# Loading the first weights ahead of later tokens, and laying the first projections one by one among the first attention steps

## The chip, the cores and the metric

The kernel runs on one core of a Trainium2 chip. The time is the device time of one execution in microseconds (us). A time of a kernel is the median over several runs. A profile is taken of one further execution, which has its own time.

## The reference

The computation is one transformer layer on 2048 tokens of width 256, all in 32-bit floats: a differential attention block and a feed-forward block, each between a layer norm in front and a layer norm behind, with the input added back. The part that the change touches is the front of the attention block.

```python
qkv = layernorm(x) @ Wqkv_w.T + Wqkv_b           # 2048 x 4096
q, k, v = split(qkv, [2048, 1024, 1024])         # 16 q heads, 8 k heads of 128; 4 v heads of 256
p1, p2 = softmax of causal (q . k) / sqrt(128)   # the two halves of each pair of heads
o = (p1 - lam * p2) @ v
o = rmsnorm(o) * subln_w * (1 - LAMBDA_INIT)
x = x + layernorm(o @ out_w.T + out_b)
```

The feed-forward block multiplies by signs, does a Walsh-Hadamard transform, and has gate, up and down matrices of 1024 hidden columns. The kernel folds the transforms into the weights.

## The kernel before, in words

**Tiling.** Tokens lie in 16 tiles of 128, and in four blocks of 512. The heads lie in four groups; a group has four q heads, two k heads and one v head of 256 columns. `qT`, `kT` and `vt` hold one group, and `xnT` holds the normalised input, transposed, with the 256 features in two chunks on the partitions.

**Stages.** Block 0 of x is loaded as four tiles, by SP and ACT in turn; blocks 1 to 3 (512 KB each) by SP, into a pool of three buffers. `load_qkv(0, ...)` loads the group's weights `wq` in four pieces of 256 KB, all from ACT's queue, in the order k, q heads 0 and 1, q heads 2 and 3, v; the v bias comes from POOL's queue. `colv` (biases and scales, 27 KB) is loaded by POOL and scaled there by `load_lambdas`, which then issues the loads of the lambdas, of `wo` and of the output bias. `norm_first` and `norm_in(b)` normalise a block on VectorE (statistics, then a power on POOL, then one subtract-and-multiply per tile). `turn_in(b)` transposes a block on TensorE in eight transposes and copies the two chunks to `xnT`, one on ACT and one on VectorE. `project_heads(g, nb, j2)` projects two heads of block nb in four matmuls of 512 columns into one PSUM tile and evicts the two halves with the bias; `j2` 0 and 1 are q, 2 is k. With `both=False` both halves are evicted by ACT, else the second by VectorE. `project_values(g, nb)` does v for a block in eight matmuls of 256 columns and one eviction on VectorE.

**Attention steps.** A unit is a token tile of one group (both halves of it for tiles 0 to 7). Each step of the main loop brings a new unit: half 0 of its `scores`, `exponentials`, then `combine` of the unit before it (which mixes the two softmaxes, transposes in blocks and sends the result through DRAM), then half 1 of the scores, then `values` (output `po`) of the unit three steps back, then `project_out`.

**What sets the order.** The order on each engine is the order in which the program issues the work; it is written out by hand. Dictionaries `before`, `mid`, `between` and `after` hold, for each step, the functions that are called at four places in it; `put` and `put_block` fill them. Around the change, `before` of step 0 runs ahead of the first scores, `mid` and `between` after `combine`, and `after` at the end of the step. Scores, projections and transposes take their PSUM tiles in turn from the pool `ps_s`, which has three buffers, so a tile waits until the tile three places earlier has been read. The pool `ps_o` has two buffers and serves `po` and `pout`. `WARM` matmuls on the identity run at the very start.

Of the kernel before, what the change touches and what calls it, by code (L numbers as in the profile page):

```python
# [10 lines left out]
F32 = mybir.dt.float32  # L11
# [5 lines left out]
P = 128  # L17
# [13 lines left out]
LAMBDA_INIT = 0.8 - 0.6 * math.exp(-0.3 * 1)  # L31
SCALE = D ** (-0.5)
LAG = 3
WARM = 12
MASKED = 1e30
HIGHEST = 3e38

# [7 lines left out]
NCOL = 54  # L45
# [3 lines left out]
def kernel(  # L49
# [14 lines left out]
    nc = tc.nc  # L64

    const = ctx.enter_context(tc.tile_pool(name="const", bufs=1))
    ident = const.tile([P, P], F32, name="ident")
    make_identity(nc, ident)

# [5 lines left out]
    mhalf = const.tile([P, 4], F32, name="mhalf")  # L75
    nc.gpsimd.memset(mhalf, -0.5)

    colv = const.tile([P, NCOL], F32, name="colv")
    nlam = const.tile([P, 1], F32, name="nlam")

    acc = const.tile([P, NT, HID], F32, name="acc")
# [1 line left out]
    def rstd_of(pool, src, n, tag):  # L83

        st = pool.tile([P, 4, 6], F32, tag="st" + tag, name="st" + tag)
        mv = pool.tile([P, 4, 2], F32, tag="mv" + tag, name="mv" + tag)
        for t in range(n):
            nc.vector.bn_stats(st[:, t, :], src[t] if isinstance(src, list) else src[:, t, :])
            nc.vector.bn_aggr(mv[:, t, :], st[:, t, :])
        ve = pool.tile([P, 4], F32, tag="ve" + tag, name="ve" + tag)  # L90
        nc.vector.tensor_scalar(ve[:, :n], mv[:, :n, 1], EPS, None, ALU.add)
        rstd = pool.tile([P, 4], F32, tag="rs" + tag, name="rs" + tag)
        nc.gpsimd.tensor_tensor(rstd[:, :n], ve[:, :n], mhalf[:, :n], ALU.pow)
        return mv, rstd

    def normalise(dst, src, mv, rstd, t):
        nc.vector.tensor_scalar(
            dst, src, mv[:, t, 0:1], rstd[:, t : t + 1], ALU.subtract, ALU.mult
        )
# [7 lines left out]
    with ExitStack() as actx:  # L107
# [6 lines left out]
        ps_s = actx.enter_context(tc.tile_pool(name="ps_s", bufs=3, space=PSUM))  # L114
        ps_o = actx.enter_context(tc.tile_pool(name="ps_o", bufs=2, space=PSUM))
# [3 lines left out]
        qT = [qkp.tile([P, NT, 2, 2, 64], F32, name=f"q{m}") for m in range(2)]  # L119
# [6 lines left out]
        xnT = xtp.tile([P, 2, S], F32, name="xnT")  # L126
        wsrc = wqkvT.rearrange("(c p) o -> p c o", p=P)
        loaded = {}

        def load_qkv(g, engine, pieces=1):  # L130

            wq = xtp.tile([P, 2, 1024], F32, tag="wq", name=f"wq_{g}")
            vb = xtp.tile([P, 256], F32, tag="vb", name=f"vb_{g}")
            step = 512 // pieces
            parts = [(512, 2048 + g * 256, 256)]
            parts += [(lo, g * 512 + lo, step) for lo in range(0, 512, step)]
            parts += [(768, 3072 + g * 256, 256)]
            for lo, at, n in parts:
                engine.dma_start(wq[:, :, lo : lo + n], wsrc[:, :, at : at + n])
            nc.gpsimd.dma_start(vb, vbias[:, ts(g, 256)].to_broadcast([P, 256]))  # L140
            loaded[g] = wq, vb

# [18 lines left out]
                    ALU.mult,  # L161
                )

        def project_heads(g, nb, j2, both=True):

            wq, _ = loaded[g]
            cols4 = ts(nb, 512)
            pp = ps_s.tile([P, 1024], F32, tag="sc", name=f"pp_{g}_{nb}_{j2}")
            for h in range(2):
                j = 2 * j2 + h  # L170
                for c in range(2):
                    nc.tensor.matmul(  # L172
                        pp[:, ts(h, 512)],
                        lhsT=wq[:, c, ts(j, P)],
                        rhs=xnT[:, c, cols4],
                        start=(c == 0),
                        stop=(c == 1),
                    )
            for h in range(2):
                j = 2 * j2 + h  # L180
                col = g * 4 + j if j < 4 else H + g * 2 + j - 4
                bias = colv[:, C_QKB + col : C_QKB + col + 1]
                src = pp[:, ts(h, 512)]
                if j < 4:
                    dst = qT[h][:, ts(nb, 4), :, j2, :].rearrange("d t s q -> d (t s) q")
                    src = src.rearrange("d (t q) -> d t q", q=64)
                else:
                    dst = kT[h][:, cols4]
                scale = -SCALE if j < 4 else 1.0
                if h == 0 or not both:  # L190
                    nc.scalar.activation(dst, src, AF.Identity, bias=bias, scale=scale)
                else:
                    nc.vector.tensor_scalar(dst, src, scale, bias, ALU.mult, ALU.add)
# [262 lines left out]
        xsm = pstack.enter_context(tc.tile_pool(name="xsm", bufs=2, side="right"))  # L456
        xts = []
        for b in range(NB):
            xt = xin.tile([P, 4, HID], F32, tag="xt", name=f"xt_{b}")
            if b:  # L460
                nc.sync.dma_start(xt, x4[b])
            else:

                for t in range(4):
                    (nc.sync, nc.scalar)[t % 2].dma_start(xt[:, t, :], x4[0][:, t, :])
                load_qkv(0, nc.scalar, pieces=2)
            xts.append(xt)
        nc.gpsimd.dma_start(colv, cols)

        def warm_up():  # L470

# [1 line left out]
            for k in range(WARM):  # L473
                nc.tensor.matmul(warm[:, :P], lhsT=ident, rhs=ident, start=True, stop=True)

        def norm_first():

            xt = xts[0]
            done = None
            for t in range(4):  # L480
                ln = rstd_of(xsm, xt[:, t : t + 1, :], 1, f"x{t}")
                if done:
                    normalise(xt[:, t - 1, :], xt[:, t - 1, :], *done, 0)
                done = ln
            normalise(xt[:, 3, :], xt[:, 3, :], *done, 0)

        def norm_in(b):
            xt = xts[b]
# [248 lines left out]
        pieces = ffn_pieces()  # L737
# [14 lines left out]
        before, mid, between, after = {}, {}, {}, {}  # L752

        def put(where, step, f, *args, **kw):
            where.setdefault(step, []).append(lambda: f(*args, **kw))

        def put_block(where, steps, g, nb, parts, both=True):
            for step, part in zip(steps, parts):
                if part == 3:
                    put(where, step, project_values, g, nb)  # L760
                else:
                    put(where, step, project_heads, g, nb, part, both=both)


        put(before, 0, warm_up)
        put(before, 0, norm_first)
        put(before, 0, load_lambdas)
        put(before, 0, turn_in, 0)
        put_block(before, [0] * 2, 0, 0, [2, 0], both=False)
        put(before, 0, norm_in, 1)  # L770
        put(before, 0, lambdas)
        put_block(before, [0], 0, 0, [1], both=False)
        put(before, 0, turn_in, 1)
        put_block(mid, [0], 0, 0, [3], both=False)
        put(mid, 0, norm_in, 2)
        put_block(mid, [0] * 2, 0, 1, [0, 1], both=False)
        put(between, 0, turn_in, 2)
        put_block(between, [0] * 2, 0, 1, [2, 3], both=False)
        put(mid, 1, norm_in, 3)
        put_block(mid, [1] * 2, 0, 2, [0, 1], both=False)  # L780
        put_block(between, [1, 1], 0, 2, [2, 3], both=False)
        put(mid, 2, turn_in, 3)
        put_block(between, [2, 3, 3, 4], 0, 3, range(4), both=False)
        put(after, 4, pstack.close)
        for g in range(1, NG):
            end = place[g, NT - 1, 0]
            put(after, end - 12, load_qkv, g, nc.sync)
            put(after, end + LAG + 2, load_wo, g)
            put(mid, end + LAG + 3, scale_wo, g)
            if g == 1:  # L790

                for nb in range(3):
                    put_block(between, [end + 5 - 2 * nb, end + 6 - 2 * nb], g, nb, [0, 1])
                put_block(before, [end] * 2, g, 3, [0, 1])
                for nb in range(4):
                    put_block(before, [end], g, nb, [2])
                    put_block(after, [end + 2], g, nb, [3])
            else:
                put_block(between, [end - 5, end - 4, end - 4, end - 3], g, 3, range(4))
                put_block(between, [end - 3, end - 3, end - 2, end - 2], g, 2, range(4))  # L800
                put_block(between, [end - 2, end - 1, end - 1], g, 1, range(3))
                put_block(after, [end - 1, end], g, 1, [3])
                put_block(before, [end], g, 0, [2])
                put_block(between, [end, end + 1], g, 0, [0, 1])
                put_block(after, [end + 2], g, 0, [3])
# [36 lines left out]
        at = lambda k: units[k] if 0 <= k < len(units) else None  # L842
# [92 lines left out]
```

## Time and profile before

| What | Value |
|---|---|
| Median of 3 runs | 1466.45 us (1466.3 to 1468.71) |
| The profiled execution's own time | 1470.85 us |
| Its span in the trace | 1469.1 us |
| Mean granted TensorE clock | 0.997 |
| TensorE busy | 1445.6 us |
| VectorE busy | 1035.0 us |
| ACT busy | 517.4 us |
| POOL busy | 359.5 us |

In the profile, PE is TensorE's matmul row, PEld its weight loads, DVE is VectorE, ACT is ScalarE, POOL is GpSimd, SP is the engine that issues most DMAs. A 32-bit matmul of the program shows as two matmuls in the trace, so `x24` is twelve of the program. A chain line has the start, the length and what ran, followed back from the last instruction of the execution. The lines are L165 to L193 for `project_heads`, L201 and L208 for `project_values`, L260 to L286 for the scores, L376 for `values`, L500 to L502 for the transposes of x.

### The profile page before, as it was taken

What the parts mean: (1) busy time and instruction counts of PE and PEld (TensorE: products, weight loads), DVE (VectorE), ACT (ScalarE), POOL (GpSimd) and SP (SyncE); (2) the same over time, 40 slices, a digit from 0 to 9 for tenths busy, and PEclk for the clock granted to TensorE, in tenths of its full rate; (3) what the DMA queues carried; (4) which work ended last, traced back from release to release, by engine and by line L of the source; (5) the groups of instructions that cost most, each with busy time, mean ns of one, the idle gap of its engine ahead of it and who ended that gap; (6) DMA issues with size and microseconds to landing.
All of it is one profiled execution on the core that took longest, in us unless ns stands there. A gap on an engine that the chain in (4) does not pass through costs nothing.

```text
span 1469.1 us, 17573 instructions
## 1 busy us (share of the span) xinstructions
PE 1445.6 (98%) x5464; PEld 1036.9 (71%) x5464; DVE 1035.0 (70%) x2408; ACT 517.4 (35%) x1121; POOL 359.5 (24%) x684
## 2 busy tenths in 40 slices
PE   8999999999999999999999999999999999999998
PEld 5567776666767677676677776675677767888887
DVE  4479788756576888744867779545877888756774
ACT  2354333323232334322433334223433454531211
POOL 2016734642006861011101111111111121121110
PEclk9999999999999999999999999999999999999999
DMA  3059899965486889831698898631999998522000
GB/s 116 22 129 193 184 200 219 175 129 117 84 186 154 159 183 210 175 91 49 137 183 176 176 203 172 140 75 30 208 205 187 199 183 174 142 76 61 29 23 15
DMA packets 494716, 204.50 MB, mean 139 GB/s; under 512 B 390960, under 2 KB 491840, under 8 KB 494624
## 3 DMA queue, kind: packets, MB, share of 16 engines
q1 hardware_dynamic: 490576, 193.65, 62.9%
q0 software_dynamic: 2512, 8.29, 2.2%
q10 hardware_dynamic: 1536, 1.44, 0.3%
q8 instruction: 45, 0.74, 0.2%
q14 instruction: 47, 0.39, 0.1%
HBM read 107.90 MB, written 95.42 MB: 138 GB/s over the span
## 4 chain that ended last, share of the span: by engine, by line
PE 91%; DVE 6%; ACT 1%; DMA 1%; issue 1%; ACTq 0%; POOL 0%; POOLq 0%; DVEq 0%
PE po L376 30%; PE sc L260 28%; PE pp L172 11%; PE pout L441 7%; PE gu L660 7%; PE pv L201 4%; PE pd L690 4%; DVE e L275 2%; DVE e L333 1%; DVE e L352 1%; DMA wq<-in_wqkvT 1%; DVE e L286 0%; PE tx L647 0%; DVE xo L420 0%; DVE cf L328 0%
## 5 line engine op out<-in xcount | busy, mean ns | idle before, releaser
L260 PE MATMUL sc<-k,q 128*128 128x512 f32 (+7 forms) x1280 | 479.5, 520 | 9.7 <-DVE last L286 3.7
L376 PE MATMUL po<-v,pt 128*128 128x256 f32 x2176 | 485.4, 379 | 0.0
L376 PEld LDWEIGHTS po<-v,pt 128*128 128x128 f32 x2176 | 425.9, 196 | 57.1 <-issue 9.3
L260 PEld LDWEIGHTS sc<-k,q 128*128 128x128 f32 x1280 | 236.5, 190 | 229.6 <-issue 183.8
L301 ACT ACTIVATE e<-e,last 128x192 f32<-128x192 f32 (+28 forms) x256 | 299.6, 1171 | 219.8 <-DVE last L286 204.2
L275 DVE TENSOR_SCALAR_CACHE_REDUCE e<-sc 128x1024 f32<-128x1024 f32 (+15 forms) x248 | 231.2, 932 | 189.6 <-PE sc L260 188.8
L401 POOL TENSOR_TENSOR u<-ss,ed 128x1 f32<-128x1 f32 (+1 forms) x96 | 18.3, 191 | 764.6 <-ACT po L390 764.4
L387 ACT COPY osb<-po 128x256 f32<-128x256 f32 (+1 forms) x96 | 42.6, 444 | 459.3 <-PE po L376 451.9
L172 PE MATMUL pp<-xnT,wq 128*128 128x512 f32 x384 | 173.2, 601 | 4.1 <-DMA wq<-in_wqkvT 2.4
L352 DVE STREAM_TRANSPOSE e<-e 128x768 f32<-128x768 f32 (+7 forms) x192 | 172.3, 937 | 6.7
L333 DVE SCALAR_TENSOR_TENSOR e<-e,cf,e 128x64 f32<-128x64 f32 (+31 forms) x128 | 173.8, 1378 | 3.4
L172 PEld LDWEIGHTS pp<-xnT,wq 128*128 128x128 f32 x384 | 73.1, 193 | 89.0 <-issue 84.3
L441 PE MATMUL pout<-wo,oT 128*128 128x256 f32 x512 | 120.9, 379 | 0.0
L275 DVE TENSOR_SCALAR_CACHE_REDUCE e<-sc,mx 128x320 f32<-128x320 f32 (+13 forms) x128 | 97.2, 759 | 21.0 <-PE sc L260 7.9
L441 PEld LDWEIGHTS pout<-wo,oT 128*128 128x128 f32 x512 | 97.3, 190 | 12.8
L673 ACT ACTIVATE hT<-gu,colv 128x256 f32<-128x256 f32 x64 | 30.4, 475 | 132.6 <-PE gu L660 91.0
L286 DVE CUSTOM_DVE_ANT_0 e<-sc,mask,mx 128x64 f32<-128x64 f32 x248 | 70.4, 284 | 8.9
L660 PE MATMUL gu<-fxnT,wgate 128*128 128x256 f32 x256 | 65.8, 379 | 0.2 <-DVE last L286 0.2
L660 PE MATMUL gu<-fxnT,wup 128*128 128x256 f32 x256 | 65.7, 379 | 0.0
L404 POOL TENSOR_SCALAR osb<-osb,f 128x256 f32<-128x256 f32 x128 | 61.3, 479 | 12.3
L402 POOL TENSOR_TENSOR f<-u,mhalf 128x1 f32<-128x1 f32 (+1 forms) x96 | 60.0, 625 | 7.5
L674 DVE SCALAR_TENSOR_TENSOR hT<-gu,colv,hT 128x256 f32<-128x256 f32 x64 | 30.9, 482 | 41.7 <-ACT hT L673 41.6
(99 smaller groups left out, 1110.9 us busy)
## 6 DMA issues: line engine op xcount, KB each, us to landing
dr<-e SPq DMA_DIRECT2D x20, 1024.0 KB, 4.7
pt<-dr SPq DMA_DIRECT2D x80, 256.0 KB, 5.9
dr<-e SPq DMA_DIRECT2D x20, 896.0 KB, 4.4
pt<-dr SPq DMA_DIRECT2D x80, 224.0 KB, 5.1
do<-xo SPq DMA_DIRECT2D x64, 256.0 KB, 3.8
oT<-do SPq DMA_DIRECT2D x256, 64.0 KB, 2.7
dr<-e SPq DMA_DIRECT2D x20, 768.0 KB, 4.3
pt<-dr SPq DMA_DIRECT2D x80, 192.0 KB, 4.6
```

The lines of the kernel that those rows point to most:

```text
L172: nc.tensor.matmul(pp[:, ts(h, 512)], lhsT=wq[:, c, ts(j, P)], rhs=xnT[:, c, cols4], start=(c == 0), stop=(c == 1),)
L260: nc.tensor.matmul(sc[:, 512 * k : 512 * k + ww], lhsT=qT[m][:, u.i, u.subs[a]].rearrange("d p q -> d (p q)"), rhs=kT[m][:, at + lo : at + ...
L275: nc.vector.tensor_scalar(dst, src, 1.0, best, ALU.mult, ALU.min, accum_out=u.mx[:, k0, c : c + 1],)
L286: nc.vector.tensor_tensor_reduce(e[:, L - 64 : L], sc[:, tail : tail + 64], mask, 1.0, best, ALU.add, ALU.min, accum_out=u.last[:, k0 : k0 ...
L301: nc.scalar.activation(e, e, AF.Exp, bias=u.last[:, 2 * a + m : 2 * a + m + 1], scale=-1.0, accum_out=u.d[:, a, m : m + 1],)
L333: nc.vector.scalar_tensor_tensor(e0, e1, cf[:, a : a + 1], e0, ALU.mult, ALU.add)
L352: nc.vector.transpose(xv[:, r], ev[:, r])
L376: nc.tensor.matmul(u.po[:, ts(a, HID)], lhsT=ptv[:, g, r, :], rhs=vt[:, kc, :], start=(kc == 0), stop=(kc == u.i),)
L402: nc.gpsimd.tensor_tensor(f[:, : u.ns], w[:, : u.ns], mhalf[:, : u.ns], ALU.pow)
L404: nc.gpsimd.tensor_scalar(u.osb[:, a, :], u.osb[:, a, :], f[:, a : a + 1], 16.0, ALU.mult, ALU.mult)
L441: nc.tensor.matmul(u.pout[:, :HID], lhsT=u.oT[:, c, p, :], rhs=wos[u.g][:, p, c, :], start=(p == 0 and c == 0), stop=(p == 1 and c == 1),)
L660: nc.tensor.matmul(ps[:, ts(2 * j + n, 256)], lhsT=ffn[which][:, c, ts(fc, P)], rhs=xnT[:, c, :], start=(c == 0), stop=(c == 1),)
```

## The change

`load_qkv` takes a list of engines and hands its pieces round; for group 0 they are issued by SP and ACT in turn, in the order q, q, k, v, directly behind block 0 of x and ahead of blocks 1 to 3. `colv` is loaded by ACT. Block 0 is normalised, transposed and in part projected in two halves of 256 tokens (`norm_first(half)`, `turn_first(half)`, `project_heads(..., n=256)`), the transposes in tiles of `ps_o`. The calls for group 0's projections are placed one by one in steps 0 to 4, in another order; with `n=256` a block number counts halves, so `project_heads, 0, 1, ..., n=256` is the second half of block 0; its k piece and one of its two q pieces come after block 1's transposes. Three pieces of block 3 are evicted by ACT and VectorE together. `WARM` goes from 12 to 10. The later groups' loads are issued by SP as before, with k behind q.

```diff
-WARM = 12
+WARM = 10
...
-        def load_qkv(g, engine, pieces=1):
+        def load_qkv(g, engines, pieces=1):
...
-            parts = [(512, 2048 + g * 256, 256)]
-            parts += [(lo, g * 512 + lo, step) for lo in range(0, 512, step)]
+            parts = [(lo, g * 512 + lo, step) for lo in range(0, 512, step)]
+            parts += [(512, 2048 + g * 256, 256)]
             parts += [(768, 3072 + g * 256, 256)]
-            for lo, at, n in parts:
-                engine.dma_start(wq[:, :, lo : lo + n], wsrc[:, :, at : at + n])
+            for k, (lo, at, n) in enumerate(parts):
+                engines[k % len(engines)].dma_start(wq[:, :, lo : lo + n], wsrc[:, :, at : at + n])
...
-        def project_heads(g, nb, j2, both=True):
+        def project_heads(g, nb, j2, both=True, n=512):
...
-                load_qkv(0, nc.scalar, pieces=2)
+                nc.scalar.dma_start(colv, cols)
+                load_qkv(0, (nc.sync, nc.scalar), pieces=2)
             xts.append(xt)
-        nc.gpsimd.dma_start(colv, cols)
...
-        def norm_first():
+        def norm_first(half):
 
             xt = xts[0]
-            done = None
-            for t in range(4):
-                ln = rstd_of(xsm, xt[:, t : t + 1, :], 1, f"x{t}")
-                if done:
-                    normalise(xt[:, t - 1, :], xt[:, t - 1, :], *done, 0)
-                done = ln
-            normalise(xt[:, 3, :], xt[:, 3, :], *done, 0)
+            lns = [rstd_of(xsm, xt[:, t : t + 1, :], 1, f"x{t}") for t in (2 * half, 2 * half + 1)]
+            for t, ln in zip((2 * half, 2 * half + 1), lns):
+                normalise(xt[:, t, :], xt[:, t, :], *ln, 0)
+
+        def turn_first(half):
+
+            xt = xts[0]
+            for c in range(2):
+                pst = ps_o.tile([P, 512], F32, tag="o", name=f"pst_0_{half}_{c}")[:, :256]
+                for t in range(2):
+                    nc.tensor.transpose(pst[:, ts(t, P)], xt[:, 2 * half + t, ts(c, P)], ident)
+                (nc.vector.tensor_copy, nc.scalar.copy)[c](xnT[:, c, ts(half, 256)], pst)
...
-        put(before, 0, norm_first)
+        put(before, 0, norm_first, 0)
+        put(before, 0, turn_first, 0)
+        put(before, 0, norm_first, 1)
         put(before, 0, load_lambdas)
-        put(before, 0, turn_in, 0)
-        put_block(before, [0] * 2, 0, 0, [2, 0], both=False)
+        put(before, 0, project_heads, 0, 0, 0, both=False, n=256)
+        put(before, 0, project_heads, 0, 0, 1, both=False, n=256)
+        put(before, 0, turn_first, 1)
+        put(before, 0, project_heads, 0, 0, 2, both=False, n=256)
         put(before, 0, norm_in, 1)
-        put(before, 0, lambdas)
-        put_block(before, [0], 0, 0, [1], both=False)
-        put(before, 0, turn_in, 1)
-        put_block(mid, [0], 0, 0, [3], both=False)
+        put(before, 0, project_values, 0, 0)
+        put(before, 0, project_heads, 0, 1, 1, both=False, n=256)
+        put(mid, 0, turn_in, 1)
         put(mid, 0, norm_in, 2)
-        put_block(mid, [0] * 2, 0, 1, [0, 1], both=False)
-        put(between, 0, turn_in, 2)
-        put_block(between, [0] * 2, 0, 1, [2, 3], both=False)
+        put(mid, 0, project_heads, 0, 1, 2, both=False, n=256)
+        put(mid, 0, project_heads, 0, 1, 1, both=False)
+        put(mid, 0, project_values, 0, 1)
+        put(mid, 0, lambdas)
+        put(mid, 0, turn_in, 2)
+        put(mid, 0, project_heads, 0, 1, 0, both=False, n=256)
+        put(between, 0, project_heads, 0, 1, 2, both=False)
+        put(between, 0, project_heads, 0, 2, 2, both=False)
         put(mid, 1, norm_in, 3)
-        put_block(mid, [1] * 2, 0, 2, [0, 1], both=False)
-        put_block(between, [1, 1], 0, 2, [2, 3], both=False)
-        put(mid, 2, turn_in, 3)
-        put_block(between, [2, 3, 3, 4], 0, 3, range(4), both=False)
+        put(mid, 1, project_heads, 0, 2, 0, both=False)
+        put(between, 1, project_heads, 0, 1, 0, both=False)
+        put(after, 1, turn_in, 3)
+        put(before, 2, project_values, 0, 2)
+        put(mid, 2, project_heads, 0, 3, 0, both=True)
+        put(mid, 2, project_heads, 0, 2, 1, both=False)
+        put(before, 4, project_values, 0, 3)
+        put(before, 4, project_heads, 0, 3, 2, both=True)
+        put(between, 4, project_heads, 0, 3, 1, both=True)
         put(after, 4, pstack.close)
...
-            put(after, end - 12, load_qkv, g, nc.sync)
+            put(after, end - 12, load_qkv, g, [nc.sync])
```

More of the change, by code (lines that the diff above doesn't have):

```diff
@@ L66 @@
     const = ctx.enter_context(tc.tile_pool(name="const", bufs=1))
+    colv = const.tile([P, NCOL], F32, name="colv")
     ident = const.tile([P, P], F32, name="ident")
@@ L76 @@
     nc.gpsimd.memset(mhalf, -0.5)
-    colv = const.tile([P, NCOL], F32, name="colv")
     nlam = const.tile([P, 1], F32, name="nlam")
@@ L162, in scale_wo @@
                 )
-        def project_heads(g, nb, j2, both=True):
+        def project_heads(g, nb, j2, both=True, n=512):
             wq, _ = loaded[g]
-            cols4 = ts(nb, 512)
-            pp = ps_s.tile([P, 1024], F32, tag="sc", name=f"pp_{g}_{nb}_{j2}")
+            cols4 = ts(nb, n)
+            nt = n // P
+            pp = ps_s.tile([P, 1024], F32, tag="sc", name=f"pp_{g}_{nb}_{j2}_{n}")
             for h in range(2):
@@ L172, in project_heads @@
                     nc.tensor.matmul(
-                        pp[:, ts(h, 512)],
+                        pp[:, 512 * h : 512 * h + n],
                         lhsT=wq[:, c, ts(j, P)],
@@ L182, in project_heads @@
                 bias = colv[:, C_QKB + col : C_QKB + col + 1]
-                src = pp[:, ts(h, 512)]
+                src = pp[:, 512 * h : 512 * h + n]
                 if j < 4:
-                    dst = qT[h][:, ts(nb, 4), :, j2, :].rearrange("d t s q -> d (t s) q")
+                    dst = qT[h][:, ts(nb, nt), :, j2, :].rearrange("d t s q -> d (t s) q")
                     src = src.rearrange("d (t q) -> d t q", q=64)
```

## The prediction

> **What bounds the kernel now.** I read the page's busy shares first, then the chain of work that ended last over the first 110 us, then the same stretch as TensorE's timeline and as windows, then the DMA issues.
>
> The page says that TensorE sets the end, and that nothing but its first few per cent can be gained without taking matmuls away.
>
> ```profile
> PE 1445.6 (98%) x5464; PEld 1036.9 (71%) x5464; DVE 1035.0 (70%) x2408; ACT 517.4 (35%) x1121; POOL 359.5 (24%) x684
> ...
> PE 91%; DVE 6%; ACT 1%; DMA 1%; issue 1%; ACTq 0%; POOL 0%; POOLq 0%; DVEq 0%
> ```
>
> The chain (start us, length us, what) shows where it isn't TensorE. From 102.16 us on it is matmuls without a break as far as I read it (200 us). Before that it starts with a weight load, and leaves TensorE at each of the three transposes of x.
>
> ```profile
> 1.67 9.65 DMA wq<-in_wqkvT
> ...
> 11.45 13.12 PE pp L172 x24
> ...
> 25.86 0.48 ACT xnT L501
> ...
> 26.37 0.70 DVE xnT L502
> ...
> 45.50 1.24 DVE v L208
> ...
> 61.84 1.23 DVE v L208
> ...
> 66.91 0.77 DVE e L352 x2
> 67.68 0.58 DVE xnT L502
> ...
> 91.28 1.74 PE po L376 x8
> ```
>
> The windows (us: busy of PE, PEld, DVE, ACT, POOL; granted clock; DMA share; GB/s) show that TensorE restarts at half clock after its pause for the weights:
>
> ```profile
> 9.40:12.90 3.50, 1.45 (x2) 0.84 (x3) 1.04 (x2) 0.27 (x1) 1.02 (x4) 0.56 1.02 333
> 12.90:16.30 3.40, 3.40 (x5) 1.35 (x4) 2.06 (x10) 0.00 (x0) 2.71 (x4) 0.50 0.76 214
> 16.30:19.70 3.40, 3.40 (x9) 1.36 (x8) 2.15 (x7) 1.27 (x2) 0.00 (x0) 0.95 0.46 175
> ```
>
> And the DMA issues of that stretch (KB each, us to landing) show who shares the engines with the weights:
>
> ```profile
> xt<-in_x SPq DMA_DIRECT2D x3, 512.0 KB, 10.9
> wq<-in_wqkvT ACTq DMA_DIRECT2D x4, 256.0 KB, 10.7
> ```
>
> **The tally of before.** I take the stretch from the first projection (11.45) to the end of the second unit's `values`, po_1 (91.28+1.74 = 93.0): 81.6 us. It holds the same matmuls in both kernels. At full clock: 12 `project_heads` at half of the chain's 6.87 us per x16 row, 3.435 each, 41.2; 4 `project_values` at 3.45, 13.8; three block transposes at 0.87, 2.6; po_0 and po_1 0.86+1.74 = 2.6; scores of units 0 to 4, 7,040 columns at 0.429 us per 512 columns and pass, two passes, 11.8. Sum 72.0. So 9.6 us of the stretch are lost: 13.12 - 24 x 0.429 = 2.8 at half clock; and, as the chain's distance between two TensorE rows less the small matmuls in it, 1.5 from 24.57 to 27.11, 1.4 from 45.48 to 47.91, 0.9 around 62 to 64, 2.2 from 64.4 to 68.3; 0.8 in latencies of 64-column scores. Ahead of it lie 11.45 us of start.
>
> **What the Trainium skill says.** "TensorE: Matmul & The Clock Gate", Part 1 (What's actually happening): the clock halves after an idle activity window of about 3.4 us and returns after a busy one, and the windows run free of the kernel's start. The trace agrees: 0.5 from about 9.5 us, back at about 16.3, some 6.8 us later. The same page, Part 4: transposes do not keep the clock up. The trace agrees in that the clock fell although transposes ran until 9.04. "DMA: Bandwidth & Descriptors", Queues, rings and completion order: the issuing queues share the same 16 engines round robin[...]. The trace agrees: the 128 KB loads of x take 2.9 to 3.1 us, the 256 KB weight loads behind them 9.6 to 11.7.
>
> **The change, part by part.** *Loads.* The four 256 KB weight pieces move ahead of blocks 1 to 3 of x, and half of them to SP's queue: SP now carries xt0, xt2, q0, k, then x blocks 1 to 3; ACT carries xt1, xt3, colv, q1, v. In before, SP's third place was x block 1, 512 KB, landed at 1.65+10.9 = 12.55. Its x loads landed at about 3.6. If 512 KB take 8.95 us there, half of it (q0) takes 4.5: landing at 8.1. The other bound is ACT's third place of before: 11.3. I take 9.3 as start of the first projection, near the middle; ACT's table load ended at 8.49 in before, so its copy of the first transposed half (0.59 for twice the columns) is no later than that. k and v follow at about 12 to 13.5, needed at 14.6 and 16.3. Gain: 11.45 - 9.3 = 2.15.
>
> *Two halves.* The first transposes need two of four token tiles. 256-column matmuls cost half of 512-column ones (`values` and `project_values` run at 3.45 us per x16, 0.216 each, with a 0.19 us weight load hidden under each), so six halves cost nothing. The second half's four transposes now fall inside the stretch: +0.5. The two warm-up matmuls dropped (four of 0.22 us) end before x is normalised: nothing.
>
> *Clock.* TensorE starts at 9.3 and goes cold at about 9.5, as before. But it is then busy through the window from 9.5 to 12.9, where before it was busy for 1.45 of 3.5 us, so I let the clock return at 12.9: loss (12.9-9.5)/2 = 1.7 instead of 2.8. Gain 1.1. Ends: nothing lost if the window falls kindly, 3.4 if the clock returns only at 16.3.
>
> *Order.* Before, each block's transposes were followed at once by work that needs their result, and small scores by work that needs their buffer. After, pieces of 1.7 to 3.4 us that need neither stand between. I walked the new order through the three score buffers of `ps_s` with the trace's durations. Against the 6.0 us of stalls and 0.8 of latencies I find: 0.5 at the second score of unit 0 (see below); 0.9 where unit 1's first score needs the buffer whose two ACT evictions (1.27 us) have just begun; 0.5 at the transposes of block 3, which wait for `norm_in(3)` behind unit 0's `combine` on DVE; 0.1 at pp of block 3 after a 1.24 us v eviction; and the 0.8 of latencies. Sum 2.8, gain 6.8 - 2.8 = 4.0.
>
> *Added waits.* `colv` goes from POOL's queue to ACT's, ahead of q1 and v. POOL's scaling of it waits for it, and behind it POOL holds the loads of lambdas, wo and outb (900 KB) and block 1's rstd. It lands sooner (before: 11.6), so those 900 KB start some 2 us sooner, into the loads of v and x block 1. SP's load of x block 1 waits for xt0 (3.6 us), and ACT's issue of v for xt1, ahead of its table load: both met early. On DVE, `norm_in(1)` now stands ahead of the first v eviction, and that ahead of unit 0's scores: this is the price of loading x later.
>
> *DVE and ACT copies.* Three second halves of block 3's pieces go from ACT to DVE (about 0.65 us each), one in step 2 and two in step 4, where TensorE gets 10.3 us of pieces and the step lasts some 16 us against DVE's some 10 of work: hidden. Without that cover it would be 2 us.
>
> **Sum.** After: 9.3 + 72.0 + 0.5 + 1.7 + 2.8 = 86.3 where before stood 93.0: -6.7. From there both run the same instructions with TensorE at the end of the chain, so it carries to the end. The profiled execution took 1470.85 us (span 1469.1), 4.4 above the median of the runs, 1466.45. Against its own time that is 1464.15. The unprofiled runs may lose less at the start than the profiled one, so I carry over 6.4: **1460.0**.
>
> **Rivals.** *The start isn't won* (0.18). q0 lands no sooner than ACT's third place of before, 11.3, and the clock returns only at 16.3. For it: the change takes no byte from the front of the queues; colv's 128 small rows join them. Against: SP's third place, not ACT's, holds q0. Start 11.4 (+2.1), cold (16.3-11.4)/2 = 2.45 (+0.75): gain 3.8, 1462.6.
>
> *The stalls move* (0.11). DVE and ACT get the same copies in a shorter time, and those 4.0 us return at other buffers. For it: scores of four units still pass through three buffers, and DVE's busy share is near 0.95 from 85 us on. Against: DVE is idle for most of 25 to 65 us. Gain 2.15 + 1.1 - 0.5 = 2.7: 1463.7, not to be told from no change.
>
> *Slower* (0.05). x block 1 comes late: it lies behind 1 MB of weights, with 900 KB of POOL's loads beside it. From its landing to the second score of unit 0 there are 4.98 us of `norm_in` (12.55 to 17.53 in before) and 1.24 of v eviction, 6.2 in all. TensorE is there at about 22, so a landing at 16 costs nothing, and each us after that one us. My estimate is 14 to 17. The gain is gone at 22.7, and it is slower by 0.2% from 25.6. For it: before, loads of this size took up to 13.3 us. Against: all of these bytes had landed by about 19 us in before.
>
> **How the numbers follow.** A measurement tells about 0.2%, 2.9 us, from no change (the three runs span 2.4). The likeliest case, 0.66, is a gain of 5 to 9 us: 1457.5 to 1461.5, its own range. Of the first rival 0.15 counts as faster, 0.03 with the second as same. Faster 0.81, same 0.14, slower 0.05. The range 1457.0 to 1464.5 takes in the first two rivals and the clock's lower end, and leaves out the slower one and a start at 7.4 with no cold clock.
>
> **What would show it.** First pp starts at 8 to 10 us in place of 11.45; granted clock 1.0 again from about 13; po_1 ends near 86; no DVE copy of xnT longer than a few tenths in the chain; the scores' wait for unit 0 under 1 us. Wrong would be: pp starting past 11, x block 1 landing past 18, a second half-clock stretch, or DVE rows of over 5 us in the chain between 30 and 90.

## The result, and the profile after

The changed kernel takes 1464.53 us (median of 20 runs, 1461.3 to 1466.21), the kernel before, timed beside it, 1467.27 us (20 runs, 1466.28 to 1469.51). The ratio is 0.9979, with a 95% interval of 0.9972 to 0.9986. The gain is 2.7 us where 6.4 were forecast.

The page of the changed kernel's profile (execution of 1462.91 us, span 1461.1) shows TensorE with 4.4 us less busy time, and the same share of the chain:

```profile
PE 1441.2 (99%) x5484; PEld 1040.1 (71%) x5484; DVE 1038.5 (71%) x2412; ACT 516.9 (35%) x1125; POOL 359.1 (25%) x683
...
PE 92%; DVE 6%; issue 1%; ACT 1%; DMA 1%; SPq 0%; POOL 0%; POOLq 0%; DVEq 0%; ACTq 0%
```

Its chain (start us, length us, what) over the stretch of the tally:

```profile
1.65 7.71 DMA wq<-in_wqkvT
...
9.50 3.69 PE pp L173 x16
...
40.47 0.24 DVE e L276 x2
...
41.19 0.97 PE sc L261 x4
...
49.90 0.39 issue
50.29 1.06 PE pst L506 x8
51.35 3.47 PE pv L202 x16
...
54.85 1.24 DVE v L209
...
63.30 1.27 ACT q L192 x2
...
83.39 1.74 PE po L377 x8
```

The first projection starts at 9.50 instead of 11.45. Two of the long pieces away from TensorE are left in this chain (an eviction of v, 1.24 us, and one of q, 1.27), with other matmuls running during most of them: TensorE is idle for 0.24 us at the first and under 0.1 at the second. po_1 ends at 83.39 + 1.74 = 85.1 instead of 93.0. From there to the end of the span are 1461.1 - 85.1 = 1376.0 us; before it was 1469.1 - 93.0 = 1376.1. So between these two executions 7.9 us were won, 1.95 ahead of the first projection and the rest in the tally's stretch (81.6 to 75.6), and nothing was given back behind it. The windows (us: busy of PE, PEld, DVE, ACT, POOL; granted clock; DMA share; GB/s) show that this execution had no half clock at all:

```profile
9.40:12.90 3.50, 3.40 (x16) 3.04 (x17) 0.25 (x1) 0.84 (x2) 2.73 (x6) 1.00 1.02 299
12.90:16.30 3.40, 3.40 (x20) 2.99 (x19) 2.59 (x10) 1.94 (x5) 0.00 (x1) 1.00 0.94 298
```

And the DMA issues (KB each, us to landing) show the weights on two queues:

```profile
wq<-in_wqkvT SPq DMA_DIRECT2D x2, 256.0 KB, 8.2
...
xt<-in_x SPq DMA_DIRECT2D x3, 512.0 KB, 9.8
...
wq<-in_wqkvT ACTq DMA_DIRECT2D x2, 256.0 KB, 9.3
```

The question is then why 7.9 us between two profiles are 2.7 us between two medians. The profiled execution of before took 1470.85 us, 3.6 over the median of its runs; that of the changed kernel 1462.91, 1.6 under. 7.9 - 3.6 - 1.6 = 2.7.

### The profile page after: what moved, and what is told of

Its sections match the earlier page's. It is cut to its first block, busy times and chain, and to the rows that moved or that the text cites. A ratio compares the mean times of both kernels' runs of the same rounds, so it can differ in the third digit from the quotient of the medians.

```text
span 1461.1 us, 17617 instructions
## 1 busy us (share of the span) xinstructions
PE 1441.2 (99%) x5484; PEld 1040.1 (71%) x5484; DVE 1038.5 (71%) x2412; ACT 516.9 (35%) x1125; POOL 359.1 (25%) x683
## 4 chain that ended last, share of the span: by engine, by line
PE 92%; DVE 6%; issue 1%; ACT 1%; DMA 1%; SPq 0%; POOL 0%; POOLq 0%; DVEq 0%; ACTq 0%
PE po L377 30%; PE sc L261 29%; PE pp L173 11%; PE pout L442 7%; PE gu L666 7%; PE pv L202 4%; PE pd L696 4%; DVE e L276 1%; DVE e L334 1%; DVE e L353 1%; DMA wq<-in_wqkvT 1%; DVE e L287 0%; PE tx L653 0%; DVE xo L421 0%; DVE cf L329 0%
## 5 line engine op out<-in xcount | busy, mean ns | idle before, releaser
L173 PE MATMUL pp<-xnT,wq 128*128 128x512 f32 (+1 forms) x408 | 170.8, 568 | 2.8 <-DMA wq<-in_wqkvT 2.6
L173 PEld LDWEIGHTS pp<-xnT,wq 128*128 128x128 f32 x408 | 76.7, 190 | 81.1 <-issue 74.6
```

What stands on the lines that cost most here:

```text
L173: nc.tensor.matmul(pp[:, 512 * h : 512 * h + n], lhsT=wq[:, c, ts(j, P)], rhs=xnT[:, c, cols4], start=(c == 0), stop=(c == 1),)
```

## Experiments

**Theory A:** the start differs from execution to execution. The clock's activity windows, of which the prediction speaks, run free of the kernel, and the change leaves TensorE idle in such a way that more executions fall to half clock. **Theory B:** the start is always as in the two profiles, and the changed kernel loses its gain elsewhere. To part them I looked at more executions, kept TensorE busy, and then moved the two suspects, loads and warm-up, each alone.

### Both kernels once more

No edit.

> The kernel before, unchanged, to see how typical its profile was. Theory A (the start differs from execution to execution: the profiled execution of before started its projections late, at 11.45 us, and ran 4.9 us of them at half clock): this profile has a first projection at 9.5 to 11 us, po_1 ends at 88 to 92 instead of 93.0, and the execution takes 1466 to 1469. Theory B (the start is always like that, and the changed kernel loses its gain later): first projection at 11.3 to 11.6, po_1 at 93 again.

> The changed kernel, unchanged. Theory A: its profile starts the first projection within 0.5 us of 9.5, but in most executions with one clock window (3.4 us) at half clock, so po_1 ends at about 86.8 (85.1 + 1.7) and the execution takes 1464 to 1465; time against before -2 to -3.5. Theory B: po_1 ends at 85 to 86, and the loss of 1.6 against the profiled execution (1462.91) is found behind 130 us.

`before_again` took 1468.37 us, ratio 0.9999 (0.999 to 1.0007), which is what two copies of one kernel should show. Its profile fell on an execution of 5463.72 us and decides nothing between the theories. `after_again` took 1464.8, ratio 0.9971 (0.996 to 0.9982). Its profile (1465.8 us) shows what the first didn't. TensorE's timeline, and the windows:

```profile
9.49 6.63 PE L173 MATMUL pp<-xnT,wq 128*128 128x256 f32 x16 [2.85 <-DMA wq<-in_wqkvT]
```

```profile
6.00:9.40 3.40, 0.55 (x3) 0.31 (x3) 2.40 (x10) 0.37 (x1) 1.41 (x3) 0.88 0.92 296
9.40:12.90 3.50, 3.41 (x8) 2.82 (x9) 0.15 (x1) 0.00 (x0) 2.64 (x6) 0.50 1.06 313
12.90:16.30 3.40, 3.40 (x13) 2.73 (x13) 0.00 (x0) 0.98 (x3) 0.00 (x0) 0.63 0.64 216
```

The first projections start at the same 9.49, and take 6.63 us instead of 3.69. The clock was at half from about 8.6 to 15.4. po_1 ends at 88.0, 2.9 later than in the first profile, not the 1.7 that I had expected of one window: it was two. 1464.0 - 88.0 = 1376.0 remain behind it, so theory B's loss behind 130 us is not there.

The mean granted clock of each execution sorts the times. For before, with 70 executions in all on three chips: 36 at 0.999 or more, with medians near 1466.8; 29 at 0.998, near 1468.5; 5 at 0.997, at 1470.1 and 1470.7. For the changed kernel, 27 executions: 5 at 0.999, median near 1462.35; 16 at 0.998, 1464.5 and 1464.8; 6 at 0.997, near 1466.1. At equal clock the change is worth about 4 us (1466.8 - 1462.35 = 4.45 without half clock, 3.7 to 4.0 at 0.998). But half of before's executions were without half clock, and 5 in 27 of the changed kernel's. The mix is not the same on each chip: 12 of 27, 6 of 17 and 18 of 26 of before's executions had 0.999 or more, and that alone moves its median from 1466.79 to 1468.45.

### TensorE kept busy

```diff
+        def keep_busy(n, name):
+
+            tile = ps_s.tile([P, 1024], F32, tag="sc", name="fill" + name)
+            for k in range(n):
+                nc.tensor.matmul(tile[:, :P], lhsT=ident, rhs=ident, start=True, stop=True)
...
         put(before, 0, turn_first, 0)
+        put(before, 0, keep_busy, 6, "a")
```

In before the same, with a tile of `ps_o`, one matmul ahead of each pair of block 0's transposes and five behind the last.

> Before, with one identity matmul ahead of each pair of block 0's transposes and five behind them, so that TensorE isn't idle while it waits for the weights. Theory A: the clock stays at 1.0, 2 to 3 us are won against before, and the times of the executions lie closer together (spread under 1.5). Theory B: under 1 us.

> The changed kernel with six identity matmuls (2.6 us) between block 0's first transposes and the first projection. Theory A: clock 1.0 in every execution, all near 1461 to 1462.5, so 1.5 to 3 us better than the changed kernel, and 3 to 5 better than before kept busy in the same way: that is the change without the clock. Theory B: no change against the changed kernel (1464.5).

`after_warm`: 1462.38 us, ratio to before 0.9954 (0.9941 to 0.9968), all five executions within 1461.93 and 1462.91. With six matmuls for nothing (1.8 us of TensorE in the profile), the changed kernel becomes about 2.4 us faster than `after_again` on the same chip, as theory A says. `before_warm`: 1467.55, ratio 0.9996 (0.9987 to 1.0004), spread 2.3. That was a miss of theory A: 2 to 3 us were expected. There are two reasons. There was less to win, since most executions of before lose less at the start than the profiled one did: 12 of 27 timed beside it show no half clock. And in the profile a second half-clock stretch stands where before stalls at the transposes of block 3 (windows, columns as above):

```profile
60.00:64.50 4.50, 2.78 (x13) 1.45 (x13) 3.98 (x17) 2.71 (x10) 0.15 (x1) 1.00 0.02 5
64.50:68.00 3.50, 3.50 (x5) 1.38 (x5) 0.00 (x0) 0.00 (x0) 0.00 (x0) 0.55 0.40 117
```

TensorE is busy for 2.78 of 4.5 us in the stall, and the next 3.4 us run at half clock. The fillers don't reach there. None of the changed kernel's profiles has a half-clock stretch between its first 16 us and the idle tail at the end.

### Loads alone, order alone

`loads_warm` is `before_warm` with the change's loads, in before's order of the pieces; `order_warm` is `after_warm` with before's loads. Beside what is shown, `load_qkv` takes a list of engines as in the change, and the fillers are as above. For `loads_warm`

```diff
-                load_qkv(0, nc.scalar, pieces=2)
+                nc.scalar.dma_start(colv, cols)
+                load_qkv(0, (nc.sync, nc.scalar), pieces=2)
...
-        nc.gpsimd.dma_start(colv, cols)
```

and for `order_warm`

```diff
-                nc.scalar.dma_start(colv, cols)
-                load_qkv(0, (nc.sync, nc.scalar), pieces=2)
+                load_qkv(0, [nc.scalar], pieces=2)
...
+        nc.gpsimd.dma_start(colv, cols)
```

> The kernel before kept busy as in before_warm, with the change's loads alone: colv on ACT, the weights ahead of blocks 1 to 3, handed to SP and ACT in turn, in before's order k, q, q, v. Theory A (the profile of before overstated the wait; weights usually land at about 9.9): first projection at 9.4 to 9.7 instead of 10.1, time 0.3 to 0.8 under before_warm. Theory B (the loads give the 2.15 us of the prediction): first projection 2 us earlier, time 2 under before_warm. Rival C: block 1 of x lands so late that its transposes wait, time above before_warm.

> The changed kernel kept busy as in after_warm, with the loads put back: all four weight pieces from ACT, blocks 1 to 3 of x from SP at once, colv on POOL; the order of the steps and the two halves stay. Theory A: first projection at 9.9 to 10.3, then the same stretch as in after_warm (9.44 to 85.07), so 0.5 to 1 above after_warm: 1463.0 to 1463.4, and 4 to 4.5 under before_warm. Theory B: 2 above after_warm, 1464.4.

> The kernel before once more, one look, since the profile of before_again fell on an execution in which TensorE ran at about a quarter of its speed for milliseconds. Theory A: first projection at 9.8 to 10.6; if the execution takes about 1466.8 its clock is 1.0 in the first 90 us, if 1468.4 there is one stretch of 3.4 us at half clock, either ahead of 20 us or in the stall near 60 us. Theory B: first projection at 11.3 to 11.6 and half clock for 4.9 us of it, as in the first profile.

`before_look` (no edit, 1467.09 us) is the execution of before that the first profile should have been. Its chain:

```profile
1.67 8.45 DMA wq<-in_wqkvT
...
10.25 10.55 PE pp L172 x24
...
87.51 1.73 PE po L376 x8
```

The weights end the wait at 10.25 instead of 11.45, and the 24 matmuls take 10.55 us instead of 13.12: full clock. po_1 ends at 89.2, 3.8 earlier than in the first profile, and 1465.3 - 89.2 = 1376.1 remain. That is what theory A said. The stretch from first projection to po_1 takes 79.0 us here and 75.6 in the changed kernel without half clock. The windows over the stretch, first `before_look`, then the changed kernel:

```profile
10.25:89.24 78.99, 74.97 (x245) 43.38 (x246) 41.57 (x152) 29.68 (x73) 8.21 (x18) 1.00 0.18 54
9.50:85.13 75.63, 74.30 (x273) 48.37 (x274) 44.11 (x157) 29.63 (x77) 8.14 (x18) 1.00 0.20 60
```

TensorE's idle time in it falls from 4.0 us (78.99 - 74.97) to 1.3.

`order_warm` took 1463.53 us, ratio 0.9968 (0.9956 to 0.9981). Its chain:

```profile
10.14 3.69 PE pp L173 x16
...
84.03 1.74 PE po L377 x8
```

It starts at 10.14, 0.7 later than `after_warm` (9.44), and po_1 ends at 84.03 + 1.74 = 85.8, 75.6 after the start, as with the new loads. So the order gives its 3.4 us with the old loads too, and between these two executions the loads give 0.7. `loads_warm` took 1466.88, ratio 0.9992 (0.9984 to 1.0), against 0.9996 for `before_warm`, with intervals that overlap. It can't price the loads: its weights had landed by about 9.0 us, but ACT's copy of the transposed x ended at 9.73 and the fillers behind that, so TensorE started at 10.07, no earlier than `before_warm` (9.99), and the start that was expected (9.4 to 9.7) did not come. Between executions at a mean clock of 0.999 the two medians are 1466.84 and 1467.10; the rest of the difference is the half clock, which 1 of 13 executions shows against 4 of 13.

### The warm-up count

```diff
-WARM = 10
+WARM = 12
```

> The changed kernel with 12 warm-up matmuls as before instead of 10; nothing else. Theory A (the change lengthened TensorE's idle stretch between warm-up and first projection, so a clock window finds it idle more often): the stretch without real matmuls shrinks from 3.4 us (6.1 to 9.5) to 2.5, half-clock executions become fewer, and the median falls by 0.7 to 1.7 against the changed kernel's 1464.5 to 1464.8, to about 1463.5. Theory B (the clock is luck that the kernel doesn't touch): 1464.5 to 1465, as the changed kernel.

`after_w12`: 1461.62 us, ratio 0.9957 (0.9944 to 0.9969). This is more than theory A had asked for. All five executions lie within 1461.24 and 1462.51. TensorE's timeline:

```profile
1.46 5.49 PE L475 MATMUL warm<-ident 128*128 128x128 f32 x24 [1.46 <-POOL ident masks.py:199]
6.74 0.72 PE L490 MATMUL pst<-ident,xt 128*128 128x128 f32 x4
7.86 3.69 PE L173 MATMUL pp<-xnT,wq 128*128 128x256 f32 x16 [0.39 <-DMA wq<-in_wqkvT]
```

The warm-up ends at 6.95 instead of 6.1, the transposes follow at once, and nothing is late by it. In this execution the weights came at 7.7 us, earlier than in `after`, `after_again` and `after_warm` (9.31 to 9.37), so part of this profile's gain is the early landing. With the old loads `before_look` and `order_warm`, on the same chip, started at 10.25 and 10.14. I ran the count in four more cases.

> The kernel before with 10 warm-up matmuls instead of 12; nothing else. Theory A (the two dropped warm-up matmuls lengthen the stretch in which the clock monitor sees an idle TensorE): warm-up ends at about 6.0 instead of 6.6, more executions at half clock, median 0.5 to 1.7 above before, 1469 to 1470. Theory B (the count doesn't matter in itself): as before, 1468.3.

> The changed kernel with 8 warm-up matmuls. Theory A: warm-up ends at about 5.2, 4.3 us ahead of the first projection, longer than a clock window of 3.41: half clock in nearly every execution, median 1465 to 1467, first projections of 16 matmuls 5 to 6.7 us instead of 3.7. Theory B: 1464.5 to 1465, as with 10.

> The changed kernel with 12 warm-up matmuls once more, for the interval and beside its neighbours. Theory A: all executions within 1461 to 1463, 6 to 7 below before. Theory B: the earlier 1461.6 was luck, 1463 to 1465.

> The changed kernel with 14 warm-up matmuls. Theory A: warm-up ends at about 7.6, the first transposes end at 8.6, still ahead of the weights at 8 to 9.4; no half clock, 1461.3 to 1462.5, as with 12, or up to 0.8 later where the weights land early. Theory B: every dropped or added warm-up matmul only moves the transposes: 1464.5 to 1465.

| Kernel | Warm-up matmuls | Median us | Ratio to before, 95% |
|---|---|---|---|
| before_w10 | 10 | 1469.26 | 1.001 (1.0002 to 1.0019) |
| before, beside it | 12 | 1466.79 | 1 |
| after_w8 | 8 | 1464.88 | 0.9979 (0.9971 to 0.9987) |
| after_again | 10 | 1464.8 | 0.9971 (0.996 to 0.9982) |
| after_w12, after_w12b | 12 | 1461.62, 1462.78 | 0.9957 (0.9944 to 0.9969), 0.9968 (0.9955 to 0.998) |
| after_w14 | 14 | 1462.54 | 0.9965 (0.9953 to 0.9978) |

`before_w10`, `after_w8`, `after_w12b` and `after_w14` ran on one chip, `after_again` and `after_w12` on two others. Two warm-up matmuls fewer cost the kernel before 1.5 us by the ratio (2.5 between the medians): all 13 of its executions had a mean clock of 0.998 or 0.997, where 18 of 26 of before, beside it, had 0.999 or more. In the changed kernel 12 and 14 are 2.1 and 2.3 us below 8 on the same chip; 10 stood at 1464.53 and 1464.8 elsewhere. Between 12 and 14, and between 8 and 10, no difference can be told. The numbers of theory A were missed twice: `after_w8` came out at 1464.88, within theory B's 1464.5 to 1465 and not in theory A's 1465 to 1467, and one of its 14 executions took 1460.77; and two of the five executions of `after_w12b` lie above 1463, with the median 4.0 below before where 6 to 7 were expected, since 18 of 26 executions of before, beside it, had no half clock. What speaks for theory A is the step between 8 or 10 and 12, and the profiles. `after_w8`'s timeline:

```profile
8.89 5.80 PE L173 MATMUL pp<-xnT,wq 128*128 128x256 f32 x16 [1.58 <-DVE vex L91]
```

These 16 matmuls take 5.80 us instead of 3.69, although the profile's clock column says 1.00 there, so the record lacks a change of the clock. `after_w8`'s clock figures can't be sorted as above, and elsewhere too a mean clock may hide a stretch; the durations show it. In `after_w12`, `after_w12b` and `after_w14` the first 16 projection matmuls run at full speed: 3.69 us, 1.97 and 1.99 for the two halves, and 4.04 with a wait for the second piece in it.

In `before_w10` the clock fell at 7.77 us and came back at 14.6:

```profile
4.36:7.77 3.41, 1.85 (x13) 1.18 (x11) 3.11 (x15) 1.28 (x1) 1.77 (x3) 1.00 0.88 206
7.77:11.18 3.41, 2.21 (x5) 1.08 (x6) 1.57 (x4) 0.58 (x1) 0.65 (x1) 0.50 1.02 334
11.18:14.59 3.41, 3.41 (x5) 1.35 (x4) 2.01 (x9) 0.00 (x0) 2.94 (x7) 0.50 0.88 265
```

Put at the moment of the fall, the windows of five profiles read alike. A recorded half clock lasts 3.41 us or twice that, so I take 3.41 us as one window:

| Execution | Clock falls at | TensorE busy (transposes too) in the 3.41 us before | in the 3.41 us after | Clock back at |
|---|---|---|---|---|
| before | 9.80 | 1.67 | 1.76 | 16.6 |
| before_w10 | 7.77 | 1.85 | 2.21 | 14.6 |
| after_again | 8.61 | 1.18 | 2.53 | 15.4 |
| before_warm | 64.85 | 1.69 | 3.41 | 68.3 |
| loads_warm | 64.45 | 1.69 | 3.41 | 67.9 |

In these five the clock falls after a window that is busy for about half or less. It comes back after a window that is busy throughout; one busy for 2.53 us was not enough. This fits the warm-up: in every stretch of 3.41 us between 1.5 and 20 us TensorE is busy for at least 3.0 us in `after_w12`, 2.7 in `after_w14` and `after_warm` and 1.9 in `after_w12b`. In the first profile of the changed kernel the least is 0.85, so whether the clock falls would hang on where a window begins.

What stays open is where exactly the limit lies, and where the windows begin, which isn't in the page. `before_look`, whose clock held, also has stretches with 1.1 us at the start and 1.7 in the stall at block 3's transposes, and `order_warm`, with no half clock in five executions, has one with 1.4. That their windows began elsewhere is not shown.

## Why the prediction was wrong

The sum was about right for the changed kernel and wrong for what it was taken from. It put po_1's end at 86.3; the two profiles of the changed kernel have 85.1 and 88.0. That is luck in part, since it has 1.7 us of half clock where these have none and 2.9. What failed is the step from there to a gain.

**Against what it was made.** The failed step is the base: the gains of 2.15 at the start and 1.1 at the clock were measured from the one profiled execution of before and carried over to the median with 0.3 taken off. That execution was the slowest kind: weights at 11.45 instead of 10.25 (1.2 us) and 24 matmuls in 13.12 instead of 10.55 (2.6 us). Both shares are in `before_look`: 93.0 - 89.2 = 3.8. The 4.4 us by which the profiled execution stood above the median had been seen, and should have been read as a warning on the start. This is also why "against its own time that is 1464.15" lies 0.4 us from the measured median: as a time of the changed kernel it was near, while before's usual time was well under the one it was taken from.

**The clock.** Forecast as a gain of 1.1 (2.8 lost before, 1.7 after). In the medians it is a loss of 1.0 to 1.7: before loses 0 to 1.7 (1466.8 against medians of 1466.8 to 1468.45), the changed kernel 2.2 to 2.5 (1462.35 against 1464.53 and 1464.8). The 2.8 itself is 2.6, since at full clock the 24 matmuls take 10.55 and not 24 x 0.429 = 10.3. I put the fall at 9.5 and let the clock return at 12.9, after one window that the projections fill. In before the fall was at 9.8; in `after_again` it came at 8.6, ahead of the first projection, so the window behind it was busy for 2.53 us only, and the clock returned at 15.4, late, as the first rival had it. "TensorE: Matmul & The Clock Gate" of the Trainium skill, Part 1 (What's actually happening), says that the window runs free and that the cold count differs from run to run; these executions agree, with 3.69 and 6.63 us for the same 16 matmuls from the same start. I cited the page and then used one phase. The page's idle window before a fall is not what these runs show: TensorE was busy for 1.18 to 1.85 us of the 3.41 before it, in `before_warm` 1.69 without a transpose among them.

**The warm-up.** "The two warm-up matmuls dropped end before x is normalised: nothing" is a second step that failed. As work they delay nothing. But they keep the clock: without them before loses 1.5 to 2.5 us, and the changed kernel, which loses 2.2 to 2.5 with 10, shows no half clock in the profiles with 12 and 14. With the 12 kept, the change was worth 4.0 us in `after_w12b` and 6.8 in `after_w12`.

**The start.** The forecast of 9.3 was near for the first profile (9.50); the base of 11.45 was not, as said. What the loads give differs with the landing. With them the first projection starts at 9.4 to 9.5 in three profiles and at 7.38 to 8.89 in the four with 8, 12 or 14 warm-up matmuls; with the old loads the weights let it start at 10.14 and 10.25, and 11.45 in the first profile. At 7.38 TensorE then waited for the second piece until 10.85. Pairs of profiles give 0.7 (`order_warm`, `after_warm`) and 2.4 (`before_look`, `after_w12`). An estimate from the medians without half clock, less the order's 3.4 us, gives 1.0 (before's 1466.8 and 1462.35), 1.9 (1466.9 and 1461.62, `after_w12`) and 0.6 to 0.8 (1466.73 and `after_w12b`, `after_w14`). 2.15 is above all of these. Why the pieces land early in some executions is open; the chips differed. That the prediction's landing times "agree" with queues served in turn is more than they show: only that loads take longer behind and beside others.

**The order.** 4.0 less 0.5 for the second half's transposes, 3.5 in all; measured 79.0 - 75.6 = 3.4 at full clock in both. The stalls that the walk through the three buffers left are near in their sizes, but not in each cause: at unit 1's first score 0.9 forecast, 0.52 idle found, ended by VectorE's reading of unit 0's scores and not by the two evictions of ACT; at block 3's transposes 0.5 and 0.4; behind v's eviction 0.1 and 0.24; at unit 0's second score 0.5, and 0.24 found at block 1's transposes, which wait for VectorE's reading of unit 0's scores. The order also removed the second place where before can fall to half clock, which I had not counted.

**Hidden and carried.** The gain carried to the end: 1376.0 behind po_1 in both profiles of the changed kernel, 1376.1 in two of before. In the first profile block 1 of x had landed by 13.8 us, when its statistics started without a wait; so the slower rival was far from its point of 22.7. The copies moved to VectorE and the new waits on SP, POOL and ACT appear nowhere in the chain.

**The rivals.** "The stalls move" has the measured gain, 2.7, by luck: its cause is refuted by the 3.4 us of the order. "The start isn't won" (3.8) is right on the clock that returns late, and wrong on the start, which came at 9.50 and not at 11.4.

In sum, at the medians: 4.45 at equal clock (an estimated 1.0 for the start, 3.4 for the order) less 1.7 for the clock is the measured 2.7, taken apart and not measured a second time; beside `after_again` it is 4.45 less 1.0, 3.5.

## What to carry to other kernels

A profile is one execution: where its own time stands several us from the median, find out which stretch differs before its rows are used, by a second profile of the unchanged kernel. Matmuls that compute nothing can hold the clock for those that do, so a warm-up's price is not its own duration but what the clock does in the wait behind it; change its length only together with that wait. Where a change is worth a few us at the start, compare executions at equal granted clock, or keep TensorE busy in both.

## What the runs showed of the hardware that I had not expected

The half clock has two lengths in these runs, one window of 3.41 us (`before_warm`, `loads_warm`) and two together (before, `after_again`, `before_w10`): after the fall the clock stayed down over windows in which TensorE was busy for 1.76, 2.21 and 2.53 us, and rose after one that was busy throughout. A fall needs no idle window: TensorE was busy for 1.18 to 1.85 of the 3.41 us before it, and in the middle of the kernel a stall was enough. The same loads land at different times: the first projection could start at 7.38 to 9.50 us in the changed kernel's profiles. And one execution of the unchanged kernel before took 5463.72 us, with the first 24 projection matmuls in 39.71 us instead of 10.55 and TensorE busy to the end, without a record of a changed clock; its cause wasn't looked for.
